# The last 48 features of a down projection: two tiles' products placed in the two halves of the TensorE array

## The chip, the core and the metric

The kernel runs as one launch on one NeuronCore of a Trainium2 chip. The metric is the device time of that launch in microseconds (us), lower is better. Engines are named as in the profile: PE is TensorE's matrix multiplication, PEld its weight loads (they overlap PE), DVE is VectorE, ACT is ScalarE, POOL is GpSimd, SP is SyncE, which here only issues DMA transfers.

## The reference, cut to what matters

The input is 4096 tokens of 256 numbers, all in 32-bit floating point. The output is a sum of three things: the input, an attention layer with its own small feed-forward network, and a mixture of experts. Both layers read the normalised input `xn`. The part that the change touches is the mixture of experts:

```python
scores = softmax(xf @ gate_w.T + gate_b)            # 8 experts
top_w, top_idx = top_k(scores, 2)                    # each token goes to 2 of them
h = silu((xf @ gw.T + gb) * (xf @ uw.T + ub))        # gw, uw: 816 x 256, per expert
acc = acc + w[:, None] * (h @ dw.T + db)             # dw: 256 x 816, per expert
```

There are 816 = 6 x 128 + 48 hidden features per expert. The 48 at the end are called the rest here. The attention is a windowed one with 8 heads of 32 features: each block of 64 queries sees 192 keys, with a softmax over them.

## The kernel before, in words

The program first normalises the tokens, computes the routing, and sorts the 8192 token-expert pairs into tiles of 128 rows (stage one, the first 83 us of the profile). The tiles are worked off in units. A pair is a unit of two tiles (256 tokens) of one expert, a single is one tile. The list `UNITS` has 34 units that always run (30 pairs and 4 singles; the singles are units 3, 7, 11 and 15) and 5 more (2 pairs, 3 singles) that run only where the routing needs them, each inside an `If`.

The second stage is a loop over the 34 units, `b` from 0 to 33. The first 32 rounds (`STEPS`) each also do the attention of four heads for 256 queries ("attends" in the code), interleaved by hand with the unit's matrix products. [...] In a round with attention PE's order is:

- `scores`: eight products with a contraction of only 32 rows, four heads in the four 32-row groups of the array, each head into its own PSUM bank (`ps`);
- `chunk(0)` and `chunk(1)`: gate and up products of 128 features each (bank `gu`), which ACT and DVE turn into `hT` (gate plus bias on ACT, times up plus bias on DVE);
- in even rounds `closing`, the attention's output projection of the two tiles before (`wo`);
- `down(b - 1)`: the down projection of the unit before, from the other one of two `hT` buffers, into bank `pe`;
- `turned(b + 1)`: transposes of the next unit's tokens; then, in the first half of the loop, products for later keys, queries or values;
- `chunk(2)`, `flip(0)` (transposes of the first tile's softmax weights `pr` into bank `pT`), `chunk(3)`, `flip(1)`, `flip_rest`, `chunk(4)`, `chunk(5)`, `glu_rest` (gate and up products of the 48 rest features in one go, bank `gr`);
- `weigh`: softmax weights times values, in four 32-column groups of the array (bank `po`).

`flip` needs what `scale` makes on DVE (line 978) from `pr`, which comes through `scores` on PE, DVE, the exponentials on ACT and sums on POOL.

In `glu_rest` the gate's 48 features come out in partitions 0 to 47 and up's in partitions 64 to 111 of the same bank. The result is written to partitions 64 to 111 of `hT[:, FCM, :]`; the other partitions of that slice are zero, set once at the start. The down weights of the rest stand in partitions 64 to 111 too, with zeros in the others. So `down` of one tile is seven products of the full 128 rows, the seventh with 80 rows of zeros. A 32-bit product is executed as two matmul records with a weight load each, so a tile shows 14 records in the profile and a pair 28.

Seven PSUM banks belong to one pool (`psm`, tag `bank`) that hands them out in turn (`po` has another pool): a tile waits for the readers of the tile that was handed out seven places before. Weight loads are issued on SP: `load_down(b + 1)` after `down(b - 1)`, `load_gu(b + 2)` at the end of round `b`. Results of a unit go from bank `pe` through DVE (plus the down bias, tile `y`) to the table `done` in HBM. In rounds 32 and 33 there is no attention. After the loop the last unit's `down` follows, then the optional units (`whole`), and then the third stage, the attention layer's feed-forward network with the gathering of the experts' results.

Of the kernel before, what the change touches and what calls it, by code (L numbers as in the profile page):

```python
# [36 lines left out]
ALU = mybir.AluOpType  # L37
# [4 lines left out]
P = 128  # L42
S = 4096
D = 256
# [6 lines left out]
E = 8  # L51
FE = 816
FCE = -(-FE // P)


REM = FE % P
REM_UP = P // 2
FM = FE - REM
# [41 lines left out]
def block_kernel(ctx: ExitStack, tc: tile.TileContext, a: dict, out: bass.AP):  # L100
# [23 lines left out]
    def bank(name):  # L124
        return psm.tile([P, G], F32, tag="bank", name=name)

    def halves(pb):
        return pb.rearrange("p (t n) -> p t n", t=2)
# [32 lines left out]
    def bcast(ap, n, at):  # L161

        shape = list(ap.shape)
        shape.insert(at, n)
        return ap.unsqueeze(at).to_broadcast(shape)
# [677 lines left out]
    def rest_of(w, xT, hT, pb, gs):  # L843

        for c in range(DC):
            lo = RW + c * P
            nc.tensor.matmul(  # L847
                pb[:, 0, :], w[:, lo : lo + P], xT[:, c, :], start=(c == 0), stop=(c == DC - 1)
            )
        g, u, at = slice(0, REM), slice(REM_UP, REM_UP + REM), BW + 2 * FCM  # L850
        nc.scalar.activation(gs[u, :], pb[g, 0, :], AF.Identity, bias=w[g, at : at + 1])
        nc.vector.scalar_tensor_tensor(
            hT[u, FCM, :], pb[u, 0, :], w[u, at : at + 1], gs[u, :], ALU.add, ALU.mult
        )

    def glu(b, f, w, xT, hT):
        n = UNITS[b][1] * P
# [10 lines left out]
    def silu(hT, lo, hi, on=slice(0, P)):  # L868
        nc.scalar.activation(hT[on, lo:hi, :], hT[on, lo:hi, :], AF.Silu)  # L869

    def results(pd, n, w, hT, order):
        for t in range(n):
            for k, f in enumerate(order):
                nc.tensor.matmul(  # L874
                    pd[:, t, :],
                    hT[:, f, t * P : (t + 1) * P],
                    w[:, f * D : (f + 1) * D],
                    start=(k == 0),
                    stop=(k == FCE - 1),
                )  # L880

    def down(b, w, hT):
        at, n, _ = UNITS[b]
        pd = halves(bank(f"pe{b}"))[:, 0:n, :]
        results(pd, n, w, hT, range(FCE))
        y = he.tile([P, TB, D], F32, tag="y", name=f"y{b}")[:, 0:n, :]
        nc.vector.tensor_tensor(y, pd, bcast(w[:, FCE * D :], n, 1), ALU.add)
        nc.sync.dma_start(out=rows(done, at, n), in_=y)

    def whole(b, w, wd, xT, hT, banks, gss, y):  # L890

        _, n, _ = UNITS[b]
        n_in = n * P
        for k, f in enumerate([FCM] + list(range(FCM))):
            pb = halves(banks[k % 3])[:, :, 0:n_in]
            gs = gss[k % 3][:, 0:n_in]
            if f == FCM:
                rest_of(w, xT, hT, pb, gs)
            else:
                chunk_of(f, w, xT, hT, pb, gs)  # L900
            if f == FCM:
                silu(hT, FCM, FCE, slice(REM_UP, REM_UP + REM))
            elif f % 2:
                silu(hT, f - 1, f + 1)
        pd = halves(banks[3])[:, 0:n, :]
        results(pd, n, wd, hT, [FCM] + list(range(FCM)))
        nc.vector.tensor_tensor(y[:, 0:n, :], pd, bcast(wd[:, FCE * D :], n, 1), ALU.add)

    def scores(i, hq):

# [50 lines left out]
    def apart(i, hq):  # L961

        xd = sp.tile([P, 2, P], F32, tag="xd", name=f"xd{i}_{hq}", bufs=1)
        of = slice(hq * P, (hq + 1) * P)
        for j in range(2):
            nc.gpsimd.tensor_tensor(
                xd[:, j, :], vts[i + j + 1][:, of], vts[i + j][:, of], ALU.subtract
            )
        return xd
# [14 lines left out]
    def flip(i, hq, j, pr):  # L984
        pb = bank(f"pT{i}_{hq}_{j}")
        for hh in range(HQ):
            nc.tensor.transpose(pb[:, hh * P : (hh + 1) * P], pr[:, hh, j, 0:P], ident)

        prT = [sp.tile([P, HQ, P], F32, tag="prT", name=f"prT{i}_{hq}_{j}"), pr[:, :, j, P:]]
        for t, m in zip(prT, (first_keys, second_keys)):  # L990
            nc.vector.tensor_tensor(
                t, pb.rearrange("p (h q) -> p h q", h=HQ), bcast(m, HQ, 1), ALU.mult
            )
        return prT
# [154 lines left out]
    for b in range(ALWAYS):  # L1149

        i, hq = b // 2 * 2, b % 2
        attends = b < STEPS
        hT = hTs[b % 2][:, :, 0 : UNITS[b][1] * P]

        def chunk(f):
            glu(b, f, gus[b], xT[b], hT)

        if b + 2 < ALWAYS:
            xs[b + 2] = gather(b + 2)
        if attends:  # L1160
            pr, nm, sums = scores(i, hq)
            xd = apart(i, hq)
        if b == 0:
            xT[0] = turned(0, xs.pop(0))
        if attends:
            exps(pr, nm, sums, 0, 3)
            merge(pr, 0)
        chunk(0)
        if attends:
            exps(pr, nm, sums, 3, 6)  # L1170
            merge(pr, 1)
            merge(pr, 2)
        chunk(1)
        if attends:
            exps(pr, nm, sums, 6, 8)
            merge(pr, 3)
        if hq == 0 and i - 2 in res:
            closing(i - 2, oTs.pop(i - 2), res.pop(i - 2))
            if i < STEPS:
                res[i] = residual(i)  # L1180
        if attends:
            scale(i, hq, pr, sums, xd)
        if b == STEPS:
            att.close()
            wf = pool(ctx, "wf", right)
            hf = pool(ctx, "hf", right, bufs=2)
            accp = pool(ctx, "accp", right, bufs=4)
            got = pool(ctx, "got", right, bufs=8)
            W1, W2 = matrix(wf, "W1", F1, DC), matrix(wf, "W2", D, FC1)
            b1 = column("b1", FC1, wf)  # L1190
            gamma, beta, b2 = (row(n, D, wf) for n in ("gamma", "beta", "b2"))

            late = pool(ctx, "late", right)
            other.update({n: late for n in range(ALWAYS, BLOCKS, 3)})
            load_unit(ALWAYS)
            for n in range(ALWAYS, BLOCKS):
                xs[n] = gather(n)
        if b == STEPS + 1:
            *_, r2 = rstd_of(mv2, root_of(mv2, NT, "b"), NT, "b")
            x2s[0] = second_loads(0)  # L1200
        if b > 0:
            down(b - 1, downs.pop(b - 1), hTs[(b - 1) % 2])
        if b == ALWAYS - 1:
            load_unit(ALWAYS + 1)
        if b + 1 < ALWAYS:
            downs[b + 1] = load_down(b + 1)
        if b + 1 < ALWAYS:
            xT[b + 1] = turned(b + 1, xs.pop(b + 1))
        else:
            for n in range(ALWAYS, BLOCKS):  # L1210
                xT[n] = turned(n, xs[n])
        g = b // TG
        if attends and g + AHEAD <= NG:
            ahead = g + AHEAD
            if b % TG == 0 and g > 0:
                for c in range(DC):
                    keys(ahead, c)
            elif ahead < NG and b % TG == 1:
                values(ahead * TG + 1, 2, False)
            elif ahead < NG and b % TG == 2:  # L1220
                values(ahead * TG + 3, 2, False)
            elif ahead < NG and b % TG == 3:
                for c in range(DC):
                    queries(ahead, c, False)
        chunk(2)
        if attends:
            if hq == 0:
                pos[i] = pso.tile([P, 2, DC, P], F32, tag="po", name=f"po{i}")
                oTs[i] = sp.tile([P, 2, DC, P], F32, tag="oT", name=f"oT{i}", bufs=1)
            prT0 = flip(i, hq, 0, pr)  # L1230
        chunk(3)
        silu(hT, 0, 2)
        if attends:
            prT1 = flip(i, hq, 1, pr)
            added = flip_rest(i, hq, xd)
        chunk(4)
        n = b - (ALWAYS - len(MAYBE))
        if n >= 0:
            flags[ALWAYS + n] = nc.values_load(used[0:1, n : n + 1], min_val=0, max_val=1)
        chunk(5)  # L1240
        silu(hT, 2, 4)
        glu_rest(b, gus[b], xT[b], hT)
        silu(hT, 4, FCM)
        silu(hT, FCM, FCE, slice(REM_UP, REM_UP + REM))
        if attends:
            for j, prT in enumerate((prT0, prT1)):
                weigh(i, hq, j, prT, pos[i])
            outputs(i, hq, pos[i], oTs[i], added)
        if b + 2 < ALWAYS:
            gus[b + 2] = load_gu(b + 2)  # L1250
# [2 lines left out]

    for b in range(ALWAYS, BLOCKS):
        nc.gpsimd.memset(xs[b], 0.0)
    down(ALWAYS - 1, downs.pop(ALWAYS - 1), hTs[(ALWAYS - 1) % 2])
    load_unit(ALWAYS + 2)
    for b in range(ALWAYS, BLOCKS):
        at, n, _ = UNITS[b]
# [116 lines left out]
```

## Time and profile before

| | |
|---|---|
| median of three runs | 1103.53 us (1101.41 to 1105.42) |
| the profiled execution | 1102.41 us |
| its span, first to last instruction | 1100.7 us |
| granted TensorE clock | 1.000 |
| PE busy | 1084.8 us of the span |
| DVE, ACT, POOL busy | 591.3, 495.3, 502.7 us |
| stage one | 0 to 83 us |
| the 32 rounds with attention | 83 to 785.6 us |
| rounds 32 and 33, the last `down`, the optional units | 785.6 to 868 us |
| feed-forward network of the attention layer, gathering, output | 868 to 1100.7 us |

The profile describes one execution; the times of the three runs have none of its detail. "Busy" is the time in which an engine had at least one instruction under way. [...] In the groups of instructions, "128\*128" are the rows and columns of the array that an instruction uses, and the idle time at the end of a line is that of the engine ahead of this group, with what ended it.

### The profile page before, as it was taken

To read this page: it belongs to the slowest core of one execution; us is meant where nothing else is said; L and a number is where in the kernel's file an instruction comes from. 1 tells how busy PE (TensorE), PEld (TensorE's weight loads), DVE (VectorE), ACT (ScalarE), POOL (GpSimd) and SP (SyncE) were. 2 spreads that over 40 slices of the span, in tenths; PEclk is the share of its full clock that TensorE was granted. 3 is DMA by queue.
4 is the path that set the end of the run, shared out by engine and by line. 5 is a ranking of instruction groups with operands and counts; after the bars stand their busy time and mean duration, and the time that the engine had idled before them with its cause. 6 is when DMAs were issued, how large, how long until landed. Compare 5 with 4: busy or idle time off the path is not lost. (4 is left out here: it accounts for less than half of the span.)

```text
span 1100.7 us, 18039 instructions
## 1 busy us (share of the span) xinstructions
PE 1084.8 (99%) x6424; PEld 868.7 (79%) x6424; DVE 591.3 (54%) x1571; ACT 495.3 (45%) x1170; POOL 502.7 (46%) x620
## 2 busy tenths in 40 slices
PE   8998999999999999999999999999999999999998
PEld 6577888887888888888888888888888666666667
DVE  6655656657566566665666666656433233323213
ACT  4526446544555546646555564465343321111110
POOL 6425544455445443654455445534213175555422
PEclk9999999999999999999999999999999999999999
DMA  9152445545445354454544554545575323333112
GB/s 291 61 234 73 139 136 172 180 141 156 152 147 194 119 187 148 170 163 155 193 149 138 179 182 140 169 150 197 176 265 205 120 77 96 96 96 96 57 58 77
DMA packets 60748, 163.37 MB, mean 148 GB/s; under 512 B 6288, under 2 KB 46608, under 8 KB 51184
## 3 DMA queue, kind: packets, MB, share of 16 engines
q1 hardware_dynamic: 54176, 144.48, 37.7%
q0 software_dynamic: 6480, 17.70, 6.2%
q8 instruction: 52, 0.85, 0.3%
q14 instruction: 40, 0.33, 0.1%
HBM read 140.28 MB, written 21.89 MB: 147 GB/s over the span
## 5 line engine op out<-in xcount | busy, mean ns | idle before, releaser
L830 PE MATMUL gu<-xsT,wg 128*128 128x256 f32 (+1 forms) x1632 | 357.4, 369 | 0.7 <-ACT xsT L822 0.7
L830 PEld LDWEIGHTS gu<-xsT,wg 128*128 128x128 f32 x1632 | 288.6, 190 | 46.2 <-DVE oT L1018 10.3
L838 ACT ACTIVATE gs<-gu,wg 128x256 f32<-128x256 f32 (+1 forms) x204 | 92.1, 454 | 291.3 <-PE gu L830 290.0
L958 POOL TENSOR_TENSOR pr<-pr 128x256 f32<-128x256 f32 x128 | 92.9, 726 | 253.6 <-ACT pr L946 253.6
L874 PE MATMUL pe<-wd,hT 128*128 128x256 f32 x896 | 199.0, 379 | 0.0
L839 DVE SCALAR_TENSOR_TENSOR hT<-gu,wg,gs 128x256 f32<-128x256 f32 (+1 forms) x204 | 95.0, 467 | 177.4 <-ACT gs L838 177.2
L874 PEld LDWEIGHTS pe<-wd,hT 128*128 128x128 f32 x896 | 170.1, 190 | 22.8
L959 POOL TENSOR_TENSOR pr<-pr,ident 128x256 f32<-128x256 f32 x128 | 126.2, 986 | 10.0
L946 ACT ACTIVATE pr<-pr,nm 128x256 f32<-128x256 f32 x256 | 126.8, 498 | 0.4
L1087 ACT ACTIVATE hf<-ph,b 128x512 f32<-128x512 f32 x64 | 44.0, 687 | 158.2 <-PE ph L1080 158.2
L1080 PE MATMUL ph<-x2T,W 128*128 128x512 f32 x256 | 111.3, 593 | 0.8 <-DVE x2T L1072 0.8
L1118 PE MATMUL pd<-W,hf 128*128 128x256 f32 x512 | 111.7, 379 | 0.0
L1118 PEld LDWEIGHTS pd<-W,hf 128*128 128x128 f32 x512 | 96.9, 190 | 13.3 <-issue 0.5
L931 DVE CUSTOM_DVE_ANT_0 pr<-ps,mask 128x256 f32<-128x256 f32 x256 | 90.8, 420 | 23.2 <-PE ps L917 23.2
L804 POOL DMA_INDIRECT xs<-xnd,token x71 | 68.8, 969 | 64.9 <-DVE paired_tiles L771 31.1
L1096 POOL DMA_INDIRECT got<-done,slot x64 | 63.3, 989 | 73.9 <-DVE acc L1109 61.2
L1080 PEld LDWEIGHTS ph<-x2T,W 128*128 128x128 f32 x256 | 48.5, 190 | 58.9 <-issue 56.8
L869 ACT ACTIVATE hT<-hT 128x512 f32<-128x512 f32 (+3 forms) x148 | 80.4, 543 | 7.6 <-DVE hT L839 4.2
L1060 POOL TENSOR_TENSOR x<-x,beta 128x1024 f32<-128x1024 f32 x8 | 18.8, 2350 | 94.4 <-DVE x L1059 94.4
L1125 DVE TENSOR_TENSOR acc<-pd,acc 128x512 f32<-128x512 f32 x16 | 11.0, 690 | 83.3 <-PE pd L1118 83.3
L978 DVE TENSOR_TENSOR pr<-pr,rec 128x1024 f32<-128x1024 f32 x32 | 39.2, 1225 | 27.7 <-POOL pr L958 27.7
L946 ACT ACT_TABLE_LOAD x31 | 39.8, 1283 | 27.5 <-DVE nm L931 27.5
(209 smaller groups left out, 1393.6 us busy)
## 6 DMA issues: line engine op xcount, KB each, us to landing
wg<-in_gate_up SPq DMA_DIRECT2D x37, 1670.5 KB, 7.1
wd<-in_down SPq DMA_DIRECT2D x37, 1024.0 KB, 5.9
done<-y SPq DMA_DIRECT2D x30, 256.0 KB, 2.2
x<-in_x SPq DMA_DIRECT2D x8, 512.0 KB, 5.6
xnd<-xn SPq DMA_DIRECT2D x8, 512.0 KB, 5.4
res<-xnd SPq DMA_DIRECT2D x16, 256.0 KB, 2.9
x1d<-res SPq DMA_DIRECT2D x16, 256.0 KB, 2.2
x<-x1d SPq DMA_DIRECT2D x8, 512.0 KB, 5.8
```

What stands on the lines that cost most here:

```text
L804: nc.gpsimd.indirect_dma_start(out=x[:, t, :], out_offset=None, in_=xnd, in_offset=bass.IndirectOffsetOnAxis(ap=token[:, i : i + 1], axis=0),)
L830: nc.tensor.matmul(pb[:, k, :], w[:, lo : lo + P], xT[:, c, :], start=(c == 0), stop=(c == DC - 1),)
L838: nc.scalar.activation(gs, pb[:, 0, :], AF.Identity, bias=w[:, gb : gb + 1])
L839: nc.vector.scalar_tensor_tensor(hT[:, f, :], pb[:, 1, :], w[:, ub : ub + 1], gs, ALU.add, ALU.mult)
L869: nc.scalar.activation(hT[on, lo:hi, :], hT[on, lo:hi, :], AF.Silu)
L874: nc.tensor.matmul(pd[:, t, :], hT[:, f, t * P : (t + 1) * P], w[:, f * D : (f + 1) * D], start=(k == 0), stop=(k == FCE - 1),)
L931: nc.vector.tensor_tensor_reduce(out=pr[:, hh, j, :], in0=ps[hh][:, j, :], in1=mask[:, kind + j, :], scale=-1.0, scalar=-LOWEST, op0=ALU.a ...
L946: nc.scalar.activation(pr[:, hh, j, :], pr[:, hh, j, :], AF.Exp, bias=nm[:, j, hh : hh + 1], scale=-1.0, accum_out=sums[:, j, hh : hh + 1],)
L958: nc.gpsimd.tensor_tensor(first, first, second, ALU.add)
L959: nc.gpsimd.tensor_tensor(second, second, bcast(ident, 2, 1), ALU.mult)
L1080: nc.tensor.matmul(ph, W1[:, c, f * P : (f + 1) * P], x2T[:, c, :], start=(c == 0), stop=(c == DC - 1),)
L1118: nc.tensor.matmul(pd[:, u, :], hT[:, f, (t + u) * P : (t + u + 1) * P], W2[:, f, :], start=(f == 0), stop=(f == FC1 - 1),)
```

## The change

The rest of a pair is laid out differently. For the first tile (columns 0 to 127 of `hT`) the 48 features are written to partitions 0 to 47, for the second tile (columns 128 to 255) to partitions 64 to 111. The host puts a second copy of the 48 rows of down weights into partitions 0 to 47. The rest's product of tile 0 then contracts over partitions 0 to 63 alone and that of tile 1 over partitions 64 to 127, and the two follow each other directly, each with a PSUM bank of its own. A single keeps a product over all 128 rows, with its features in partitions 0 to 47.

The rest's product moves from the end of a tile's sum to its start, and away from the other six: in rounds 1 to 31 it stands directly behind `scores` of the next round, in the later rounds behind `chunk(0)`, there directly ahead of the other six, which it also precedes after the loop and in `whole`. `glu_rest` and its silu move ahead of `chunk(5)`. DVE's product of gate and up for the rest becomes two instructions for a pair, and the sum with the bias too (one for each bank).

In round 0, `flip(0)` moves behind `chunk(3)`, with `chunk(4)` behind it; nothing else of the attention moves.

```diff
 def rest_of(w, xT, hT, pb, gs):
     ...
-        nc.vector.scalar_tensor_tensor(
-            hT[u, FCM, :], pb[u, 0, :], w[u, at : at + 1], gs[u, :], ALU.add, ALU.mult
-        )
+        for t in range(hT.shape[2] // P):
+            to, cols = (u if t else g), slice(t * P, (t + 1) * P)
+            nc.vector.scalar_tensor_tensor(
+                hT[to, FCM, cols], pb[u, 0, cols], w[u, at : at + 1], gs[u, cols], ALU.add, ALU.mult
+            )
...
+    def silu_rest(hT):
+        silu(hT, FCM, FCE, slice(0, REM_UP + REM if hT.shape[2] > P else REM))
+
+    def results_rest(pds, w, hT):
+        for t, pd in enumerate(pds):
+            half = slice(t * REM_UP, (t + 1) * REM_UP) if len(pds) > 1 else slice(0, P)
+            nc.tensor.matmul(
+                pd,
+                hT[half, FCM, t * P : (t + 1) * P],
+                w[half, FCM * D : FCE * D],
+                start=True,
+                stop=False,
+            )
+
+    def results(pds, w, hT):
+        for t, pd in enumerate(pds):
+            for f in range(FCM):
+                nc.tensor.matmul(
+                    pd,
+                    hT[:, f, t * P : (t + 1) * P],
+                    w[:, f * D : (f + 1) * D],
+                    start=False,
+                    stop=(f == FCM - 1),
+                )
...
+    def summed(y, pds, w):
+        for t, pd in enumerate(pds):
+            nc.vector.tensor_tensor(y[:, t, :], pd, w[:, FCE * D :], ALU.add)
+
+    def down_rest(b, w, hT):
+        pds = [bank(f"pe{b}_{t}")[:, 0:D] for t in range(UNITS[b][1])]
+        results_rest(pds, w, hT)
+        return pds
...
             pr, nm, sums = scores(i, hq)
             xd = apart(i, hq)
+        if 0 < b < STEPS:
+            pds = down_rest(b - 1, downs[b - 1], hTs[(b - 1) % 2])
...
         chunk(0)
+        if b >= STEPS:
+            pds = down_rest(b - 1, downs[b - 1], hTs[(b - 1) % 2])
+            down(b - 1, pds, downs.pop(b - 1), hTs[(b - 1) % 2])
...
-        if b > 0:
-            down(b - 1, downs.pop(b - 1), hTs[(b - 1) % 2])
+        if 0 < b < STEPS:
+            down(b - 1, pds, downs.pop(b - 1), hTs[(b - 1) % 2])
...
-            prT0 = flip(i, hq, 0, pr)
+            if b:
+                prT0 = flip(i, hq, 0, pr)
         chunk(3)
         silu(hT, 0, 2)
         if attends:
+            if b == 0:
+                prT0 = flip(i, hq, 0, pr)
+                chunk(4)
             prT1 = flip(i, hq, 1, pr)
             added = flip_rest(i, hq, xd)
-        chunk(4)
+        if b:
+            chunk(4)
...
+        glu_rest(b, gus[b], xT[b], hT)
+        silu(hT, 2, 4)
+        silu_rest(hT)
         chunk(5)
-        silu(hT, 2, 4)
-        glu_rest(b, gus[b], xT[b], hT)
         silu(hT, 4, FCM)
-        silu(hT, FCM, FCE, slice(REM_UP, REM_UP + REM))
...
-            rest(down, None),
+            rest(down, down),
```

More of the change, by code (lines that the diff above doesn't have):

```diff
@@ L869, in silu, with down @@
         nc.scalar.activation(hT[on, lo:hi, :], hT[on, lo:hi, :], AF.Silu)
-    def results(pd, n, w, hT, order):
-        for t in range(n):
-            for k, f in enumerate(order):
+    def silu_rest(hT):
[13 more added lines that the diff above has]
+            for f in range(FCM):
                 nc.tensor.matmul(
-                    pd[:, t, :],
+                    pd,
                     hT[:, f, t * P : (t + 1) * P],
                     w[:, f * D : (f + 1) * D],
-                    start=(k == 0),
-                    stop=(k == FCE - 1),
-                )
-    def down(b, w, hT):
+                    start=False,
+                    stop=(f == FCM - 1),
+                )
+    def summed(y, pds, w):
[5 more added lines that the diff above has]
+        return pds
+    def down(b, pds, w, hT):
         at, n, _ = UNITS[b]
-        pd = halves(bank(f"pe{b}"))[:, 0:n, :]
-        results(pd, n, w, hT, range(FCE))
+        results(pds, w, hT)
         y = he.tile([P, TB, D], F32, tag="y", name=f"y{b}")[:, 0:n, :]
-        nc.vector.tensor_tensor(y, pd, bcast(w[:, FCE * D :], n, 1), ALU.add)
+        summed(y, pds, w)
         nc.sync.dma_start(out=rows(done, at, n), in_=y)
@@ L901, in whole @@
             if f == FCM:
-                silu(hT, FCM, FCE, slice(REM_UP, REM_UP + REM))
+                silu_rest(hT)
             elif f % 2:
                 silu(hT, f - 1, f + 1)
-        pd = halves(banks[3])[:, 0:n, :]
-        results(pd, n, wd, hT, [FCM] + list(range(FCM)))
-        nc.vector.tensor_tensor(y[:, 0:n, :], pd, bcast(wd[:, FCE * D :], n, 1), ALU.add)
+        pds = [banks[k][:, 0:D] for k in (3, 1)[:n]]
+        results_rest(pds, wd, hT)
+        results(pds, wd, hT)
+        summed(y, pds, wd)
     def scores(i, hq):
@@ L1239, in block_kernel @@
             flags[ALWAYS + n] = nc.values_load(used[0:1, n : n + 1], min_val=0, max_val=1)
+        glu_rest(b, gus[b], xT[b], hT)
+        silu(hT, 2, 4)
+        silu_rest(hT)
         chunk(5)
-        silu(hT, 2, 4)
-        glu_rest(b, gus[b], xT[b], hT)
         silu(hT, 4, FCM)
-        silu(hT, FCM, FCE, slice(REM_UP, REM_UP + REM))
         if attends:
@@ L1255, in block_kernel @@
         nc.gpsimd.memset(xs[b], 0.0)
-    down(ALWAYS - 1, downs.pop(ALWAYS - 1), hTs[(ALWAYS - 1) % 2])
+    last = hTs[(ALWAYS - 1) % 2][:, :, 0 : UNITS[ALWAYS - 1][1] * P]
+    pds = down_rest(ALWAYS - 1, downs[ALWAYS - 1], last)
+    down(ALWAYS - 1, pds, downs.pop(ALWAYS - 1), last)
     load_unit(ALWAYS + 2)
@@ L1313, in rest @@
         m = np.zeros((E, P, up.shape[-1]), np.float32)
+        m[:, :REM] = gate[:, FM:]
         m[:, REM_UP : REM_UP + REM] = up[:, FM:]
-        if gate is not None:
-            m[:, :REM] = gate[:, FM:]
         return m
```

## The prediction

> **What bounds the kernel now.** The page comes first: which engine is busy all the time.
>
> ```profile
> span 1100.7 us, 18039 instructions
> PE 1084.8 (99%) x6424; PEld 868.7 (79%) x6424; DVE 591.3 (54%) x1571; ACT 495.3 (45%) x1170; POOL 502.7 (46%) x620
> ```
>
> PE is busy for all but 16 us. An average can hide stages with other limits, so next come the busy times by stretch. Of the rounds with attention, this is the half from round 1 on:
>
> ```profile
> core 0: us, PE busy (x) PEld busy (x) DVE busy (x) ACT busy (x) POOL busy (x), PEclk, DMA share, GB/s
> 101.90:436.50 334.60, 334.60 (x2260) 280.10 (x2256) 212.08 (x562) 181.44 (x463) 158.20 (x199) 1.00 0.47 157
> ```
>
> PE has no idle time at all there, at a clock of 1.00; DVE is busy for 63%. The stretch up to 785.60 looks the same. So in these rounds a PE slot saved is time saved, until another engine is late. The waits of PE name the one place where it is late now:
>
> ```profile
> engine line waited for: us in total, times, longest us
> PE pT L987 <- DVE pr L978: 2.3, 1, 2.3
> ```
>
> One wait, and the timeline of PE shows where: round 0, behind `chunk(2)`. Columns: start, duration, engine, line, operation.
>
> ```profile
> 89.41 1.89 PE L830 MATMUL gu<-xsT,wg 128*128 128x256 f32 x8
> 93.59 0.63 PE L987 MATMUL pT<-ident,pr 128*128 128x128 f32 x4 [2.29 <-DVE pr L978]
> 94.05 1.89 PE L830 MATMUL gu<-xsT,wg 128*128 128x256 f32 x8
> ```
>
> "Busy" does not mean that the array streams at its full rate, and here that matters. The timeline of PE over a round of two pairs (round 28, even):
>
> ```profile
> 697.80 1.15 PE L917 MATMUL ps<-kt,qt 32*128 32x256 f32 x16
> 698.88 3.72 PE L830 MATMUL gu<-xsT,wg 128*128 128x256 f32 x16
> 702.44 1.89 PE L1031 MATMUL wo<-Wo,oT 128*128 128x256 f32 x8
> 704.16 6.21 PE L874 MATMUL pe<-wd,hT 128*128 128x256 f32 x28
> 710.21 0.60 PE L817 MATMUL pts<-ident,xs 128*128 128x128 f32 x4
> ...
> 718.65 1.03 PE L847 MATMUL gr<-xsT,wg 128*128 128x256 f32 x4
> 719.61 0.43 PE L1009 MATMUL po<-prT,vt 128*32 128x128 f32 x8
> ```
>
> Read the distances of starts. `pe`: 28 records in 710.21 - 704.16 = 6.05 us, so 0.216 us for one record of 256 columns: a slot. `ps`: 16 records in 698.88 - 697.80 = 1.08 us, where 16 slots would be 3.46. Four products of 32 rows run side by side: 4 slots (0.864) and 0.22 us more. `gu` behind it: 16 records in 3.56 us, 0.10 more than 16 slots. `gr` ahead of `po`: 0.96 for 4 records, again 0.10 more. The extra time lies at each change of the array's division, and the weight loads show it too, as gaps ahead of the first load in another division, which elsewhere runs ahead under the matmul before:
>
> ```profile
> 719.61 0.16 PEld L1009 LDWEIGHTS po<-prT,vt 128*32 128x32 f32 x8 [0.33 <-issue]
> ...
> 720.62 0.74 PEld L917 LDWEIGHTS ps<-kt,qt 32*128 32x128 f32 x16 [0.20 <-issue]
> 721.69 0.73 PEld L830 LDWEIGHTS gu<-xsT,wg 128*128 128x128 f32 x4 [0.33 <-DVE oT L1018]
> ```
>
> So a stretch in a division of its own pays about 0.10 for its first weights, which are not loaded ahead, and 0.10 at its end until the array is empty.
>
> **The change part by part.**
>
> *The rest's products, rounds 1 to 31.* The units summed there are 0 to 30, of which 3, 7, 11, 15 are singles: 27 pairs. Each loses 4 of its 28 `pe` records, 4 x 0.216 = 0.864 us. It gains a stretch of its own between `scores` and `chunk(0)`: two products in different row halves and banks, side by side as the four heads, so 2 slots = 0.432, plus the fixed part of a stretch. The trace has no division into 64 rows; the nearest row is `ps`, whose 1.08 us less two slots is 0.65. Below: the change from 32 to 64 rows costs nothing, 0.44. Above: nothing overlaps, 1.08.
>
> [...] The rows say 0.33 and 0.20 us of gap at each new division. [...] By the rule and the rows' price it saves 0.864 - 0.65 = 0.215. I take the latter: 27 x 0.215 = **5.8 us**.
>
> *The later pairs.* Units 31, 32, 33 and the one optional pair that runs (14 of its `whole` records are the down product of one tile, 28 those of a pair; 56 stand there, with two singles) have the rest between full-array products. There the stretch also causes a drain ahead of it and a reload behind it that are not paid today: 0.65 + 0.20 = 0.85 against 0.864. 4 x 0.01: nothing.
>
> *Singles.* The rest stays two full-array records; it moves from the sum's end to behind `scores`, and takes over the reload that `chunk(0)` pays. Nothing.
>
> *Round 0.* `chunk(3)`, 8 slots = 1.73 us, now runs inside the wait of 2.29. The rest of it, 0.56, stays: L978 ends when it did. Below nothing: DVE now has the third chunk's product ahead of `flip(0)`'s two masks, 0.48 us later than it might, and `weigh` follows 1.7 us earlier; by adding DVE's rows from L978's end (93.45) I get the last mask ready at about 99.7, where `weigh` wants it at 99.8. So up to a few tenths could be given back. I take **1.7 us**.
>
> *DVE and ACT.* L852, 0.49 us for 48x256, becomes two of 0.36 (the row of a single, 48x128); the sum with the bias, 0.69 for 128x512, becomes two of about 0.42 (L1018 is of that size). That is 0.38 us of DVE per pair, in rounds where DVE idles for a third. I cost it at nothing; uncovered it would be 30 x 0.38 = 11 us. Its cover is the time from `gr` to the rest's product. These are ACT's rows behind `gr` now:
>
> ```profile
> 719.22 0.62 ACT L869 ACTIVATE hT<-hT 128x512 f32<-128x512 f32 x1
> 719.87 0.47 ACT L851 ACTIVATE gr<-gr,wg 48x256 f32<-48x256 f32 x1
> 720.36 1.07 ACT L869 ACTIVATE hT<-hT 128x512 f32<-128x512 f32 x2
> ```
>
> The chain is ACT 0.47, DVE 2 x 0.36, silu 0.5, with the other silu (0.62) between: 2.3 us. PE has `chunk(5)` 1.73, `po` 1.01 and `ps` 1.08 = 3.8 us before it wants the result. In a single's round `chunk(5)` is half, so 2.95 against about 2.3. Behind the wait on ACT stands `chunk(0)`, and behind that everything; but it should be over. `gs` of chunk 5 now queues on ACT behind this silu, and its bank is wanted by the next `chunk(0)`: it is free about 1 us after `chunk(5)` ends, and wanted 2.7 us after that end (`po`, `ps` and the new stretch lie between).
>
> *Banks.* A pair takes two `pe` banks right behind `scores`' four; by turns of seven they are those of `gu` 4 and `gr`, free by then. `chunk(1)` gets the first `ps` bank, which DVE has read 0.84 us after `scores`, long before the 2.4 at which PE comes. Nothing.
>
> *Distance from `scores` to `flip(0)`.* It shrinks by 0.215. From the timelines, L978 ends 1.85 to 5.5 us ahead of `pT` in rounds 1 to 31. No new wait.
>
> *DMA.* No transfer is added; `wd` keeps its 1024 KB. It is now wanted at the start of a round and not in its middle, still some 30 us after its issue, and lands in 5.9. The `y` store on SP, with `load_down` behind it, waits for DVE as before. `load_gu` is released by chunk 5's product instead of the rest's, both at the round's end.
>
> **Sum.** 5.8 + 1.7 = 7.5 us. Against the profiled execution, 1102.41 (span 1100.7 and 1.7 around it), that is 1094.9. The median of the runs is 1103.53, 1.1 above that execution; the forecast for the median is 1103.53 - 7.5 = 1096.0.
>
> **The rivals.**
>
> *Cheap switch.* From 32 to 64 rows no drain, and the first weights loaded ahead. For it: within `ps` the second four loads do run ahead of their matmuls. Against: every change of division in the trace has its gap. It gives 27 x 0.42 + 4 x 0.2 + 1.7 = 13.8: 1089.7. With the reload alone saved or the drain alone: about 1093.
>
> *Passes in line.* A product is two records. [...] If both records of tile 0 must come before those of tile 1, only the second of the one overlaps the first of the other: 3 slots, section 0.87, saving nothing per pair and costing 0.2 in the four later ones. `ps` speaks against it: eight products in that order would be 9 slots, 1.94 us, and 1.08 are measured, so there the records go four abreast. Two abreast is not in the trace. Total -0.8 + 1.7: 1102.6, no change.
>
> *No overlap, slower.* The two halves are executed one after the other, 4 slots and 0.22 for the stretch: 1.08 against 0.864, in 27 pairs +5.8; in the later four 0.42 each, +1.7; round 0 gives 1.7 back. 1103.53 + 5.8 = 1109.3. It decides from a section of about 0.92 us on (27 x 0.06 = 1.7), and measurably so from 1.02. For it: the 64-row division was never seen here. Against: `ps` and `po` both run four abreast in 32-bit, with a bank per row group as the change has it.
>
> *Late features.* If ACT's silu came over 1.5 us later than reckoned, PE would stand still behind `scores`. No row hints at it; it is in the same tail.
>
> **How the numbers follow.** 0.3% of the time (3.3 us) is about what a measurement of this kernel can tell from no change. Chances: my forecast with a section of 0.6 to 0.7 us 0.66; the cheap switch, wholly or in part, 0.14; passes in line 0.09; no overlap or late features 0.11. The first two are faster: 0.80; the third the same: 0.09; the last slower: 0.11. The range takes in the first two with the runs' scatter of 2 us, 1089.5 to 1100.5, and leaves out the last two, 2 in 10.
>
> **What would show it.** In the changed profile: 12 records per tile at the sum's line; a line for the rest's products with 64\*128, whose first start is 0.65 us ahead of `chunk(0)` (0.44, 0.87 or 1.08 for the rivals); rounds with a pair before them shorter by 0.2 us; the wait of `pT` at 0.5 to 0.6 us; PE without idle time from round 1 on. A wait of the rest's product or of `chunk(0)` for ACT or DVE would make it wrong, as would a round that is no shorter.

## The result, and the profile after

The changed kernel takes 1093.91 us in the median of four runs (1093.56 to 1094.16), the kernel before in the same comparison 1103.31 (1101.41 to 1105.42). The ratio is 0.9918 with a 95% interval of 0.9905 to 0.9932: faster by 7.5 to 10.5 us. From profile to profile it is 1102.41 to 1094.16, 8.25 us.

The page of the changed kernel's profile: PE is busy 5 us less, and still for 99% of the span.

```profile
span 1092.4 us, 18151 instructions
PE 1079.8 (99%) x6424; PEld 855.0 (78%) x6424; DVE 598.3 (55%) x1633; ACT 500.7 (46%) x1170; POOL 503.3 (46%) x620
```

The busy times by stretch, for all rounds from 1 on; they begin at 99.96 now:

```profile
core 0: us, PE busy (x) PEld busy (x) DVE busy (x) ACT busy (x) POOL busy (x), PEclk, DMA share, GB/s
99.96:431.79 331.83, 331.83 (x2261) 274.40 (x2257) 214.06 (x585) 184.08 (x463) 158.35 (x199) 1.00 0.46 158
431.79:777.39 345.60, 345.60 (x2334) 292.17 (x2330) 225.23 (x616) 197.71 (x484) 169.87 (x212) 1.00 0.48 165
```

PE has no idle time in them, and DVE is busy for 65% of them. The 31 rounds took 785.60 - 101.94 = 683.66 us and take 677.43. No other engine has taken PE's place. The timeline of PE in round 28:

```profile
690.52 1.15 PE L947 MATMUL ps<-kt,qt 32*128 32x256 f32 x16
691.59 0.70 PE L883 MATMUL pe<-wd,hT 64*128 64x256 f32 x4
692.23 3.72 PE L832 MATMUL gu<-xsT,wg 128*128 128x256 f32 x16
695.78 1.89 PE L1061 MATMUL wo<-Wo,oT 128*128 128x256 f32 x8
697.51 5.34 PE L894 MATMUL pe<-wd,hT 128*128 128x256 f32 x24
702.69 0.60 PE L819 MATMUL pts<-ident,xs 128*128 128x128 f32 x4
```

The new stretch lasts 692.23 - 691.59 = 0.64 us for four records that would be 0.86 one after the other. The sum has 24 records, 5.18 us instead of 6.05: 0.216 us from start to start, where one of these records lasts 0.379 us, so that neighbours overlap in the rows. The weight loads around it (PEld, a round later) show one more gap than before, 0.33 us ahead of the first load in the division of 64 rows:

```profile
713.10 0.74 PEld L947 LDWEIGHTS ps<-kt,qt 32*128 32x128 f32 x16 [0.20 <-issue]
714.17 0.30 PEld L883 LDWEIGHTS pe<-wd,hT 64*128 64x128 f32 x4 [0.33 <-ACT hT L873]
714.81 0.30 PEld L832 LDWEIGHTS gu<-xsT,wg 128*128 128x128 f32 x2 [0.33 <-DVE nm L961]
```

The names behind the arrows are the last semaphores, not the reason: that silu on ACT was done at 712.15, 2 us before. Round 0 on PE:

```profile
89.15 3.62 PE L832 MATMUL gu<-xsT,wg 128*128 128x256 f32 x16
93.25 0.66 PE L1017 MATMUL pT<-ident,pr 128*128 128x128 f32 x4 [0.48 <-DVE pr L1008]
93.75 1.89 PE L832 MATMUL gu<-xsT,wg 128*128 128x256 f32 x8
```

The wait is 0.48 us where it was 2.29. And one wait is new, after the loop; the line of ACT is the silu that ends it, at 814.85 + 1.19 = 816.04:

```profile
813.93 1.89 PE L832 MATMUL gu<-xsT,wg 128*128 128x256 f32 x8
816.09 0.77 PE L883 MATMUL pe<-wd,hT 64*128 64x256 f32 x4 [0.27 <-ACT hT L873]
...
814.85 1.19 ACT L873 ACTIVATE hT<-hT 128x512 f32<-128x512 f32 x2
```

Where the 8.3 us between the two spans lie, from the starts of the same instructions in both timelines:

| stretch | before | after | difference |
|---|---|---|---|
| to the first `ps` (stage one) | 83.00 | 82.75 | -0.25 |
| round 0 | 18.93 | 17.21 | -1.73 |
| rounds 1 to 31 | 683.66 | 677.43 | -6.23 |
| from there to the first `ph` | 82.66 | 82.86 | +0.20 |
| from the first `ph` to the end | 232.44 | 232.15 | -0.29 |

6.23 us are 27 times 0.231: a round with a pair before it is shorter by that (round 28: 22.81 to 22.58), one with a single before it is as long as it was.

### The profile page after: what moved, and what is told of

It reads as the page before. It is cut to its first block, busy times and chain, and to the rows that moved or that the text cites. A ratio compares the mean times of both kernels' runs of the same rounds, so it can differ in the third digit from the quotient of the medians.

```text
span 1092.4 us, 18151 instructions
## 1 busy us (share of the span) xinstructions
PE 1079.8 (99%) x6424; PEld 855.0 (78%) x6424; DVE 598.3 (55%) x1633; ACT 500.7 (46%) x1170; POOL 503.3 (46%) x620
## 5 line engine op out<-in xcount | busy, mean ns | idle before, releaser
L832 PE MATMUL gu<-xsT,wg 128*128 128x256 f32 (+1 forms) x1632 | 362.5, 369 | 0.7 <-ACT xsT L824 0.7
L894 PE MATMUL pe<-wd,hT 128*128 128x256 f32 x768 | 171.6, 379 | 0.0
L894 PEld LDWEIGHTS pe<-wd,hT 128*128 128x128 f32 x768 | 145.4, 190 | 20.5 <-issue 1.0
L1008 DVE TENSOR_TENSOR pr<-pr,rec 128x1024 f32<-128x1024 f32 x32 | 39.2, 1226 | 27.3 <-POOL pr L988 27.3
```

Of the source, the lines that this page charges most:

```text
L832: nc.tensor.matmul(pb[:, k, :], w[:, lo : lo + P], xT[:, c, :], start=(c == 0), stop=(c == DC - 1),)
L894: nc.tensor.matmul(pd, hT[:, f, t * P : (t + 1) * P], w[:, f * D : (f + 1) * D], start=False, stop=(f == FCM - 1),)
```

## The experiments

My theory: a pair saves the four slots of its rest and pays two slots and about 0.2 us for a division of the array of its own, and the features are there in time; round 0 gains a chunk. The rivals: the gain comes from where the rest stands, from the separate banks or the reordering; the price is not that of the division; what round 0 gains is given back. In three profiles the granted clock is lower for a part of the span: in `same_half` it is 0.83 from 10 to 20 us and 0.997 over all, in `rest_at_sum` and `round0_alone` it is 0.998 and 0.997 over all. So I compare rounds with each other and not spans.

### full_rows: both products over all 128 rows

```diff
-            half = slice(t * REM_UP, (t + 1) * REM_UP) if len(pds) > 1 else slice(0, P)
+            half = slice(0, P)
```

> The changed kernel, but the rest's two products of a pair contract over all 128 rows, at the same new place and in the same two banks. Theory (two products side by side in 2 slots plus a fixed price of a division of its own): the stretch between scores and chunk(0) grows from the 0.63 us measured in the changed kernel to 4 slots = 0.86 us, rounds with a pair before them grow by 0.23 us, 27 times: 6.2 us, so 1100.1 us. Rival (the gain comes from moving the rest ahead, from separate banks or from the new order of glu_rest): it stays at 1094.

Measured: 1100.89 us (1100.15 to 1103.94), ratio to the kernel before 0.9978 (0.9969 to 0.9987). Its PE timeline in round 28:

```profile
695.65 1.15 PE L947 MATMUL ps<-kt,qt 32*128 32x256 f32 x16
696.72 1.13 PE L883 MATMUL pe<-wd,hT 128*128 128x256 f32 x4
697.69 3.62 PE L832 MATMUL gu<-xsT,wg 128*128 128x256 f32 x16
```

0.97 us for the stretch, and 3.45 for `gu`, which no longer pays for its first weights; the round is 22.81 again. New place, separate banks and new order are worth nothing for the rounds. The gain in them is the side-by-side execution.

### same_half: both products in the same half

```diff
-            half = slice(t * REM_UP, (t + 1) * REM_UP) if len(pds) > 1 else slice(0, P)
+            half = slice(0, REM_UP) if len(pds) > 1 else slice(0, P)
```

> The changed kernel, but both of a pair's rest products use partitions 0 to 63, so that they cannot run side by side; the second tile's 48 features are left out by it. Theory (what is bought is that the two halves run at the same time; a division of its own costs 0.20 us): 4 slots and 0.2 in the stretch between scores and chunk(0), 1.06 us instead of 0.63; 27 x 0.43 and 4 x 0.43 more, 1107.2 us: slower than before. Rival (half the rows make a product cheaper by themselves): 1094 as now.

Measured: 1107.28 us (1106.51 to 1108.84), ratio 1.0031 (1.0019 to 1.0043), slower than before. Round 28:

```profile
702.04 1.15 PE L947 MATMUL ps<-kt,qt 32*128 32x256 f32 x16
703.12 1.13 PE L883 MATMUL pe<-wd,hT 64*128 64x256 f32 x4
704.17 3.72 PE L832 MATMUL gu<-xsT,wg 128*128 128x256 f32 x16
```

1.05 us: four slots and the fixed part, and a round of 23.01. This is what the prediction's slower rival (no overlap) described. Products of 64 rows are no cheaper here by themselves than those of 128: 1.05 us less the 0.2 are 0.21 us for each of the four records, against a slot of 0.216.

### rest_at_sum: the rest's product ahead of the other six

```diff
-        if 0 < b < STEPS:
-            pds = down_rest(b - 1, downs[b - 1], hTs[(b - 1) % 2])
...
         if 0 < b < STEPS:
+            pds = down_rest(b - 1, downs[b - 1], hTs[(b - 1) % 2])
             down(b - 1, pds, downs.pop(b - 1), hTs[(b - 1) % 2])
```

> The changed kernel, but in rounds 1 to 31 the rest's two half-row products stand directly ahead of the other six (behind closing or chunk(1)), not behind scores. Theory (each change of the array's division costs about 0.1 us to empty it and 0.1 us for weights that are not loaded ahead): the stretch keeps its 0.63 us but causes another 0.2 us around it, so that a pair saves 0.03 us instead of 0.23: 27 x 0.2 = 5.4 us, 1099.4 us. Rival (the price of a division is paid once per round wherever it stands): 1094.

Measured: 1099.66 us (1098.75 to 1101.64), ratio 0.9970 (0.9963 to 0.9977). Round 28:

```profile
700.80 1.89 PE L1061 MATMUL wo<-Wo,oT 128*128 128x256 f32 x8
702.62 0.70 PE L883 MATMUL pe<-wd,hT 64*128 64x256 f32 x4
703.26 5.45 PE L894 MATMUL pe<-wd,hT 128*128 128x256 f32 x24
```

The stretch is the same 0.64, but `wo` ahead of it takes 1.82 instead of 1.73, and in the same timeline the 24 records behind it take about 0.1 more than 5.18. The round is 22.78: 0.20 longer than in the changed kernel, 0.03 shorter than before. Standing behind `scores` is what makes the change pay: there the weight loads have their gap already in the kernel before (0.33 us ahead of `gu`, in the rows of the prediction).

### rows32: the division of scores

```diff
-            half = slice(t * REM_UP, (t + 1) * REM_UP) if len(pds) > 1 else slice(0, P)
+            half = slice(t * REM_UP, t * REM_UP + 32) if len(pds) > 1 else slice(0, P)
```

> The changed kernel, but the rest's products of a pair contract over the first 32 rows of each half; 16 of the 48 features are left out. They then have the division of scores, behind which they stand in rounds 1 to 31. Theory (it is the change from 32 to 64 rows that costs 0.20 us): the first weights are loaded ahead, the stretch falls from 0.63 to 0.44 us, 27 x 0.2 = 5.3 us less, 1088.6 us. Rival (the 0.20 us come with any new bank, waiting semaphore or stationary operand, or with the return to full rows): 0.63 us and 1094 as now.

Measured: 1089.74 us (1088.25 to 1092.4). Round 28, first PE, then the weight loads:

```profile
685.74 1.15 PE L947 MATMUL ps<-kt,qt 32*128 32x256 f32 x16
686.71 0.60 PE L883 MATMUL pe<-wd,hT 32*128 32x256 f32 x4
687.24 3.72 PE L832 MATMUL gu<-xsT,wg 128*128 128x256 f32 x16
```

```profile
685.74 0.74 PEld L947 LDWEIGHTS ps<-kt,qt 32*128 32x128 f32 x16 [0.20 <-issue]
686.49 0.41 PEld L883 LDWEIGHTS pe<-wd,hT 32*128 32x128 f32 x4
687.24 0.94 PEld L832 LDWEIGHTS gu<-xsT,wg 128*128 128x128 f32 x5 [0.33 <-issue]
```

The gap ahead of the rest's loads is gone: they start 0.22 us ahead of their matmul, under the last heads. From the first `ps` to `gu` it is 1.50 us instead of 1.71, and the round is 22.38 instead of 22.58. So going from 32 to 64 rows costs the 0.2 us here (1.71 less 1.50); place, banks and columns are the same in both, and only the rows differ.

### features_late: the rest's features behind chunk(5) again

```diff
-        glu_rest(b, gus[b], xT[b], hT)
-        silu(hT, 2, 4)
-        silu_rest(hT)
         chunk(5)
+        silu(hT, 2, 4)
+        glu_rest(b, gus[b], xT[b], hT)
         silu(hT, 4, FCM)
+        silu_rest(hT)
```

> The changed kernel, but glu_rest and the rest's silu stand behind chunk(5) as before, the rest's silu after the other one. Theory (the chain from gr over ACT, DVE and ACT is 2.3 us, with the other silu about 2.5; PE reaches the rest's product 2.1 us after gr): a wait of 0 to 0.4 us of the rest's product for ACT in each of 27 rounds, and about 2.4 us once after the loop, where nothing covers it: 1097 to 1106 us. Rival (the cover is ample, the reordering was not needed): 1094 to 1096.5, only the place after the loop longer.

Measured: 1096.61 us (1095.8 to 1098.37). The rounds are as long as in the changed kernel (round 28: 22.58), only round 1 is 0.08 longer. After the loop:

```profile
814.94 1.03 PE L849 MATMUL gr<-xsT,wg 128*128 128x256 f32 x4
817.88 0.77 PE L883 MATMUL pe<-wd,hT 64*128 64x256 f32 x4 [1.92 <-ACTq L1305]
```

1.92 us instead of 0.27. So the part of my theory that saw a risk in the rounds was too careful: `po` and `ps` alone cover the chain. But the cover is not ample, as the rival had it. In the rounds behind a pair the last silu ends 0.14 to 0.15 us ahead of the rest's product (in round 1 it ends so late that PE waits), where in the changed kernel the rest's silu is done 2 us ahead. In the spans, 1094.1 to 1092.4, the reordering earns 1.7 us, once, for the last unit; the medians are 2.7 apart, but two of the four runs of `features_late` had a mean clock of 0.998 (what that means stands under `round0_alone`); the other two took 1095.8 and 1096.12 us.

### round0_as_before and round0_alone

The first undoes the change of round 0, the second makes it alone in the kernel before:

```diff
-            prT0 = flip(i, hq, 0, pr)
+            if b:
+                prT0 = flip(i, hq, 0, pr)
         chunk(3)
         silu(hT, 0, 2)
         if attends:
+            if b == 0:
+                prT0 = flip(i, hq, 0, pr)
+                chunk(4)
             prT1 = flip(i, hq, 1, pr)
             added = flip_rest(i, hq, xd)
-        chunk(4)
+        if b:
+            chunk(4)
```

> The changed kernel with round 0's transposes back at their old place. Theory (one chunk of 8 slots runs inside the wait): the wait of pT in round 0 is 2.2 to 2.3 us again, round 0 is 1.7 us longer, 1095.6 us. Rival (what is gained in round 0 is given back by later waits of round 0 or 1): 1094, with round 1 shorter by what round 0 loses.

Measured: 1097.29 us (1097.05 to 1099.61), 3.4 more than the changed kernel and twice what was expected. The timeline of round 0, and the busy times with the granted clock (PEclk) around it:

```profile
93.19 0.63 PE L1017 MATMUL pT<-ident,pr 128*128 128x128 f32 x4 [2.29 <-DVE pr L1008]
93.65 2.99 PE L832 MATMUL gu<-xsT,wg 128*128 128x256 f32 x8
96.44 1.06 PE L1017 MATMUL pT<-ident,pr 128*128 128x128 f32 x4
```

```profile
core 0: us, PE busy (x) PEld busy (x) DVE busy (x) ACT busy (x) POOL busy (x), PEclk, DMA share, GB/s
90.00:93.10 3.10, 0.90 (x5) 0.44 (x3) 1.43 (x2) 0.80 (x3) 2.94 (x4) 1.00 0.00 0
...
94.30:97.70 3.40, 3.40 (x12) 2.81 (x11) 3.37 (x8) 1.00 (x2) 1.61 (x2) 0.50 0.03 6
97.80:102.00 4.20, 4.20 (x21) 3.53 (x19) 2.26 (x5) 3.39 (x7) 0.88 (x2) 1.00 0.07 22
```

The wait is back at 2.29. But behind it the clock is halved for 3.4 us: the chunk that takes 1.73 elsewhere takes 96.44 - 93.65 = 2.79. The lost 1.7 us come on top of the wait. The profile of the kernel before has the same wait and no such drop (a clock of 1.00 from 93.50 to 97.70), so it does not come every time.

> The kernel before with the change of round 0 alone. Theory (one chunk runs inside the wait): round 0 is 1.72 us shorter in the profile, at most 1101.7 us in the median; and less if some runs of the kernel before pay for the wait a second time, by a TensorE clock that drops to half for 3.4 us behind it, as the profile of round0_as_before shows it (1.7 us): down to 1100.9, with a narrower scatter. Rival (given back by later waits): 1103.4.

Measured: 1100.23 us (1099.75 to 1102.08), against 1103.45 (1101.57 to 1106.19) of the kernel before in the same comparison: ratio 0.9971 (0.9960 to 0.9982), 3.2 us in the median, where round 0 in its profile (17.20 instead of 18.93) explains 1.73. Nothing is given back: round 1 is 22.81 as before. The rest goes with the clock. Every run has a mean granted clock, also those without a kept trace, and 3.4 us at half clock lower it by about 0.0015, by my estimate from the span: the profile of `round0_as_before` has 0.998, those of `same_half`, `rest_at_sum` and `round0_alone` 0.997 or 0.998, the seven others 0.999 or 1.000. Of the kernel before, 42 of 63 runs have 0.998 or less, of `round0_as_before` 6 of 7, of `round0_alone` 1 of 7, of the changed kernel none of 4. Among the runs of this comparison with 0.999 or more, the medians are 1101.91 and 1100.21: 1.70 apart, which is about the wait alone. Where in such a run the drop fell, these means don't show.

### around_paired and around_scores: the rest in the row groups of scores

`rows32` points to a version that leaves nothing out. Tile 0's features lie in partitions 0 to 47, so 32 of them fill row group 0 and 16 lie in group 1; tile 1's in groups 2 and 3. From round 2 on, a pair's first pieces stand ahead of `scores`, the second ones behind. The two pieces of a tile share a bank, and the kernel keeps them apart in time: a memset of one column on DVE waits for the first, and the second waits for it.

```diff
+    def results_quarter(pds, w, hT, k, behind=None):
+        for t, pd in enumerate(pds):
+            lo = t * REM_UP + k * 32
+            i = nc.tensor.matmul(
+                pd,
+                hT[lo : lo + 32, FCM, t * P : (t + 1) * P],
+                w[lo : lo + 32, FCM * D : FCE * D],
+                start=(k == 0),
+                stop=False,
+            )
...
+        if not k:
+            seen = small.tile([P, 1], F32, tag="seen", name="seen")
+            i = nc.vector.memset(seen, 0.0)
...
+        packs = 1 < b < STEPS and UNITS[b - 1][1] > 1
+        if packs:
+            pds = [bank(f"pe{b - 1}_{t}")[:, 0:D] for t in range(2)]
+            first = results_quarter(pds, downs[b - 1], hTs[(b - 1) % 2], 0)
         if attends:
             pr, nm, sums = scores(i, hq)
             xd = apart(i, hq)
-        if 0 < b < STEPS:
+        if packs:
+            results_quarter(pds, downs[b - 1], hTs[(b - 1) % 2], 1, first)
+        elif 0 < b < STEPS:
             pds = down_rest(b - 1, downs[b - 1], hTs[(b - 1) % 2])
...
-        for j in range(2):
+        for j, heads in ((0, (1, 3)), (0, (0, 2)), (1, (1, 3)), (1, (0, 2))):
             lo = (i + j) % TG * P
-            for hh in range(HQ):
+            for hh in heads:
```

The last four changed lines are in `around_paired` alone; `around_scores` keeps the order of the heads.

> The changed kernel, but from round 2 on a pair's rest product is cut into its first 32 rows and the other 16 (with 16 rows of zeros), each in a 32-row group: the first pieces of both tiles stand ahead of scores, the second ones behind, and scores takes its heads two and two, so that two heads run beside each half of the rest. Nothing is left out. A small DVE memset between them orders the two pieces that share a bank. Theory (the price is the change from 32 to 64 rows, and the four row groups are filled side by side): scores and rest together take 6 slots and 0.22 us, 1.52 us instead of 1.71; 26 x 0.19 = 5 us less, 1089. Rival (the second pieces wait for the memset, which DVE does behind other work, or the groups don't mix): 1.71 us or more, 1094 or slower.

Measured: 1092.62 us (1091.25 to 1093.2); ratio to the kernel before 0.9893 (0.9876 to 0.9909), where the changed kernel had 0.9918; span 1089.5 instead of 1092.4. Of the kernels here that leave nothing out it has the shortest span and the lowest median, by 1.3 us against the changed kernel, in another comparison. PE in round 28:

```profile
688.35 0.48 PE L903 MATMUL pe<-wd,hT 32*128 32x256 f32 x2
688.36 0.48 PE L977 MATMUL ps<-kt,qt 32*128 32x256 f32 x2
688.66 0.38 PE L903 MATMUL pe<-wd,hT 32*128 32x256 f32 x2
688.68 1.01 PE L977 MATMUL ps<-kt,qt 32*128 32x256 f32 x12
689.33 0.43 PE L903 MATMUL pe<-wd,hT 32*128 32x256 f32 x2
689.53 0.38 PE L977 MATMUL ps<-kt,qt 32*128 32x256 f32 x2
689.59 0.38 PE L903 MATMUL pe<-wd,hT 32*128 32x256 f32 x2
689.90 3.72 PE L832 MATMUL gu<-xsT,wg 128*128 128x256 f32 x16
```

Two records of the rest and two of `scores` start together, and all of it takes 1.55 us. A round with a pair before it is shorter by 0.155 and not 0.19: the memset ends at 689.21, the second pieces' weights are loaded from 689.26 on, and their second records start 0.06 us after their slot. And in the rounds of the four singles about 0.28 us is lost again (18.99 us, where 18.87 less 0.155 would be 18.71): two rows of PE in round 11 show 0.48 us between starts that lie 0.22 apart elsewhere.

```profile
341.91 0.40 PE L1069 MATMUL po<-prT,vt 128*32 128x128 f32 x8
342.39 0.43 PE L1069 MATMUL po<-pr,vt 128*32 128x128 f32 x8
```

There the mask on DVE that `po` needs ends at 342.34. In the changed kernel it ended 0.37 us ahead of `po`; a round whose own products are half as long has no more slack for `scores` that end 0.4 us later. 26 x 0.155 less 4 x 0.28 is 2.9 us, the difference of the spans.

> The same with the heads of scores in their old order, four at a time. If matmuls start strictly in program order, the first head's product waits for the rest's first piece in its row group and the other three heads wait with it: 8 slots and 0.22 us, 1.95 us, 26 x 0.24 = 6 us more than the changed kernel, 1100. If each row group takes its own products as soon as it is free: 6 slots, 1.52 us, 1089.

Measured: 1093.24 us (1092.28 to 1093.83), ratio 0.9902 (0.9883 to 0.9920). Round 28 begins so:

```profile
689.18 0.48 PE L903 MATMUL pe<-wd,hT 32*128 32x256 f32 x2
689.20 0.49 PE L977 MATMUL ps<-kt,qt 32*128 32x256 f32 x2
689.50 0.38 PE L903 MATMUL pe<-wd,hT 32*128 32x256 f32 x2
```

From the first start, 689.18, to `gu` at 690.79 it is 1.61 us; held to the order of the code it would be 8 slots and 0.22, 1.95, by my estimate. Two records of `scores` start at 689.20, 0.02 us after the rest's first pieces, which hold the row groups of heads 0 and 2. The rows don't name the heads; I take them for 1 and 3, whose groups are free, while 0 and 2 wait for the rest's pieces in theirs. So in this stretch products did not wait for those of other row groups that stand ahead of them in the code.

## Why the prediction was right

*PE bounds the rounds, and a slot saved is time saved.* Right: no idle time from round 1 on in either profile.

*The stretch.* I took 0.65 from `ps` less two slots; it is 0.64, and a pair saves 0.231 instead of 0.215. 27 of them are 6.23 instead of 5.8 us. Of the two ways to count, the one with the 0.2 us was right; without them a pair would have saved 0.864 - 0.44 = 0.42, in all 11.4 us. That a change from 32 to 64 rows has a price no run had shown when I took the 0.215, and the rule I took it by is shown by no run. What the runs show in its place is `rows32`: `scores` and rest together take 1.50 us without this change, 1.71 with it. That half of the price is the time until the array is empty was my reading of the rows, which show the 0.10 us alone.

*Two abreast.* The trace of before did not show it; it holds, since `same_half` costs 0.41 us more for the same four records.

*The later pairs: nothing.* The stretch and its 0.2 us around it came as reckoned (behind `chunk(0)` of round 33 the stretch is 0.63, the 16 records ahead of it take 3.55 instead of 3.46 and the 24 behind it 5.28 instead of 5.18), but "nothing" is the step that missed a wait. I had counted the cover of the silu chain for the rounds, `chunk(5)`, `po` and `ps`. After the loop `po` and `ps` are missing: `chunk(5)` alone covers 1.73 us from its start at 813.93, the rest's silu ends 2.11 us after that start, and PE is idle for 0.27 us. From round 32 to the first `ph` it is 0.20 us more in all. The chain itself I had summed too long: from ACT's start on `gr` (814.36) to the end of the silu it is 1.68 us and not 2.3, since the other silu runs beside DVE's two products instead of between.

*DVE and ACT at nothing.* Right. The cover would have been enough in the old order too, by 0.14 us, as `features_late` showed, except in round 1 and after the loop.

*Round 0: 1.7 us.* Right in the profile, 1.73, with nothing given back. As a term of the median it was too small: `round0_alone` measured 3.2. I had counted the wait and not a clock drop, which the profile of `round0_as_before` shows behind this wait and with which the mean of most runs of the kernel before agrees (0.998 or less in 42 of 63). With 3.2 for it and 6.2 for the pairs the sum is 9.4, which is what the medians differ by; I had 7.5. Against the profile of before, which has no drop behind the wait, 8.25 was measured. My forecast for the median, 1096.0, was 2.1 us too high, and 1.5 us of that are this term.

*Slack ahead of flip(0).* Right for this change: the least of it is 1.84 us, in round 16, where L1008 (L978 before) ends that long ahead of `pT`. That `po` behind a single's round is the tighter place, I had not looked for; only `around_paired` ran into it.

## What to carry to other kernels

Half-array products paid here where they shared a change of division that the program makes anyway: behind another divided stretch a pair saved 0.23 us, between full products 0.03. In the same division as its neighbour the stretch saved the change too, another 0.20 us a round in `rows32`. For a reordering, check its cover at every place where the code runs, the one behind the loop first: that is where the only new wait was.

## What the runs showed of the hardware that I had not expected

A wait of 2.29 us on PE cost twice in one profile. In that of `round0_as_before` the granted clock behind it is 0.50 for 3.4 us, from 94.30 to 97.70, and eight slots take 2.79 us instead of 1.73. In the profile of before the same wait had no such drop. These are the 3.41 us ahead of the drop, then the stretch of before that lies the same way to its `pT`, which starts 0.40 us later there (columns as in the table of `round0_as_before`):

```profile
90.88:94.29 3.41, 1.12 (x8) 1.07 (x8) 1.85 (x2) 0.47 (x1) 2.67 (x3) 1.00 0.00 0
...
91.28:94.69 3.41, 1.12 (x8) 1.07 (x8) 1.85 (x2) 0.47 (x1) 2.67 (x3) 1.00 0.00 0
```

The two rows agree in every figure: PE is busy for 1.12 of 3.41 us in both, and behind one the clock fell, behind the other it stayed at 1.00. So how busy PE was around this wait did not decide it alone. What did, these profiles do not show.

Row groups went ahead on their own. In `around_scores`, with four heads issued in a row and two of their groups still busy with the rest, two records of `scores` started 0.02 us after the rest's, and the whole took 1.61 us where the order of the code would have taken 1.95 by my estimate. So between row groups PE did not keep the order of the code in this stretch.
